# A selective scan beside two convolution stages: one projection tile a block at fixed places, and every fourth odd product on VectorE

## The chip, the cores and the metric

The kernel runs on one core of one Trainium2 chip. The metric is device time in microseconds of one launch, the median of the runs shown. A core has five engines that run side by side, each through its own queue of instructions in program order: TensorE (PE in the profile), VectorE (DVE), ScalarE (ACT), GpSimd (POOL) and SyncE (SP), whose queue issues all DMAs here. An instruction waits for semaphores that other engines' instructions raise, and whatever stands behind it in the same queue waits with it.

## The reference

Sixteen images of 64 x 64 pixels with 96 channels go through two residual layers. The first normalizes in groups, resamples by a Fourier method, applies two matrices with a quadratic between them, and resamples back. The second is a selective scan in four directions:

```python
xz = jnp.einsum('bhwc,pc->bhwp', x, in_proj_w)
xc, z = (xz[..., :d], xz[..., d:]); z = silu(z)
...
xc = silu(depthwise_conv3x3(xc) + conv_b)
xs = jnp.stack([x0, x1, x0[..., ::-1], x1[..., ::-1]], axis=1)
x_dbl = jnp.einsum('bkdl,kcd->bkcl', xs, x_proj_weight)
...
delta = jax.nn.softplus(dts + dt_bias)
def step(h, inps):
    dt, ut, bt, ct = inps
    h = jnp.exp(dt[..., None] * As) * h + (dt * ut)[..., None] * bt
    y = jnp.einsum('bkdn,bkn->bkd', h, ct)
    return h, y
```

There are 192 inner channels and 16 states a channel; the scan runs over 4096 positions. The sum of the four directions is normalized over channels, gated with z and projected back to 96 channels.

## The kernel before, in words

The work has three parts. **front** makes an image's first layer, the convolution and the silus, and leaves xs (the input of the scan) and z in HBM. **scan** is the long loop. **finish** takes the y of an image, normalizes, gates and projects it. front of image 1 runs alone, then scan over all images; front of the next image and then finish of the one before run in small steps beside the scan of an image. finish of the last image runs alone at the end.

The scan goes in 128 steps: 16 images, each with two pairs of directions (the forward pair, L807, and the backward pair, L809) and four chunks of T = 1024 positions. A step has six **blocks** (L621) of 64 channels, a block four **units** j = 0 to 3, of four states each; a unit fills 128 partitions (32 channels by four states) twice, e = 1 (odd) and e = 0 (even). So an image has 192 units and 48 blocks, and the whole 3072 units.

For a unit, `drive` (L795, GpSimd) forms b = dtu x bt over both halves; `decay` (L789, ScalarE) forms da = exp(delta x a) in PSUM, one tile for each half; `recur` (L801, VectorE) runs the scan h = da x h + b; then h is multiplied with ct, and `read_out` (L817, PE) sums over the states. The even scan writes into PSUM over da, and VectorE multiplies (L979). The odd scan has two ways. Mostly it writes into SBUF over b, and GpSimd multiplies it into a tile `odd` (L968). In some units ("odd_here", L952) it writes over da in PSUM as the even one does, and VectorE multiplies at once (L958). A credit decides: 7 are added in each unit, and at 30 a unit is taken; a unit can also be taken ahead of its turn, with 30 paid later (below). `keep` (L811) saves the last column of h for the next chunk, on VectorE for odd halves that GpSimd multiplies, on ScalarE otherwise.

Program order in a unit n: odd scan, its product or none, decay of the odd half of n + 1, slot 0, a store of y, GpSimd's odd product, drive of n + 2, even scan, read_out of n - 1, slot 1, even product, decay of the even half of n + 1, slot 2. b has four buffers, odd two, dtu two. dtu of the next block is fetched from HBM at j = 0 (L946), delta's halves at j = 1 and 2 (L948).

The **slots**, three a unit and 576 an image, hold everything else (L887). In each, `Background` (L860) compares how many steps a generator has made with its pace, and makes one if it is due: `front` and `finish` at SLICES = 499 in 576, where a step that yields HEAVY counts double, and `project` (L640) at 71 steps in 72 slots, two in a slot where a light step is late. `project` makes delta and dtu for the next step: six tiles of 128 x 512 (three channel groups v, two halves t). For each half it fetches three u, mixes them with three matmuls (pp), adds a bias (pr, L674), stores the rows of B and C, and then for each v makes a matmul s (L681), six ScalarE operations for the softplus (L689 to L696), four matmuls that add the pieces (L701), the product dtu with u on VectorE (L706), a copy of delta on ScalarE (L707), and two stores (L710, L711). pp and s share one PSUM bank.

front's convolution has 12 tiles an image. At the end of each it yields WAIT (L507); behind it stand two silus (L509, L510), with a load of their activation table in front and a load of the usual table behind (L511). Such a step is let through, a gate, at slot 2 of any unit where no store is pending; the next unit is then taken as odd_here, and for two slots `project` makes no BUSY steps.

Of the kernel before, what the change touches and what calls it, by code (L numbers as in the profile page):

```python
# [45 lines left out]
F32 = mybir.dt.float32  # L46
# [25 lines left out]
SLICES = 499  # L72
WAIT = -1
BUSY = -2
HEAVY = 2
PSLICES = 71
SHARE = 30
GAIN = 7
# [3 lines left out]
def tile_two_blocks(  # L82
# [159 lines left out]
    def front(mi):  # L242
# [227 lines left out]
        for i, n, tiles, both in ((1, 64, 4, 4), (0, 128, 8, 0)):  # L470
# [44 lines left out]
            yield HEAVY  # L515
            if i == 0:
                yield from parts(made["xs"][1], col)
            else:
                for p, t0 in halves:
                    to = made["xs"][2, 64:128, :].rearrange("c (w h) -> c w h", h=HW)  # L520
                    for w0 in range(0, HW, 16):
                        nc.sync.dma_start(
                            out=to[:, w0:w0 + 16, 8 * t0:8 * t0 + 32],
                            in_=col[p:p + n].rearrange("c (w h) -> c w h", w=HW)[:, w0:w0 + 16, :],
                        )
                        yield HEAVY

    def finish(mi):
# [16 lines left out]
        for _ in range(2):  # L545
            yield HEAVY
        tail = None
        for t in range(8):
# [7 lines left out]
            for ob, n in ((0, 128), (1, 64)):  # L556
# [26 lines left out]
                yield HEAVY  # L583
# [18 lines left out]
            yield HEAVY  # L602
# [4 lines left out]
            yield HEAVY  # L607
# [10 lines left out]
        for _ in tail:  # L618
            yield HEAVY
# [6 lines left out]
    def scan():  # L626


        with ExitStack() as es:
            pj = es.enter_context(tc.tile_pool(name="sc_pj", bufs=1))  # L630
            up_ = es.enter_context(tc.tile_pool(name="sc_u", bufs=4))
            cp = es.enter_context(tc.tile_pool(name="sc_bc", bufs=5))
# [7 lines left out]
            def project(mi, pair, lc, out, ps, half=None, own=None):  # L640

                if not out:
                    out["rows"] = dctx.tile([2, 2 * NS, T], F32, name="rows")
                    out["delta"] = [dctx.tile([128, T], F32, name=f"delta_d{v}") for v in range(3)]
                    out["dtu"] = [dctx.tile([128, T], F32, name=f"dtu_d{v}") for v in range(3)]
                    out["made"] = 0
                rows = out["rows"]  # L650
                xs_d = image[mi]["xs"]
                order = (0, 2, 1)
                halves = range(0, T, TB) if half is None else (half,)

                def make(name):
                    return own(name) if own else pj.tile([128, TB], F32, name=name)

                def fetch_u(v, t):
                    uv = own(f"u{v}") if own else up_.tile([128, TB], F32, name="u")
                    nc.sync.dma_start(out=uv, in_=xs_d[v, :, lc * T + t:lc * T + t + TB])  # L660
                    return uv

                ahead_u = [fetch_u(v, halves[0]) for v in order]
                for _ in range(4):
                    yield
                for t in halves:
                    u, ahead_u = dict(zip(order, ahead_u)), []
                    pp = ps.tile([128, TB], F32, name="pp", tag="g")
                    for v in range(3):
                        nc.tensor.matmul(pp, lhsT=xpt_s[:, pair, v, :], rhs=u[v], start=(v == 0), stop=(v == 2))  # L670
                    yield
                    yield BUSY
                    pr = make("pr")
                    nc.scalar.activation(pr, pp, AF.Identity, bias=bumps_s)  # L674


                    for i, v in enumerate(order):
                        if i == 0:
                            yield
                        s = ps.tile([128, TB], F32, name="s", tag="g")  # L680
                        nc.tensor.matmul(s, lhsT=dtw_s[:, pair, v, :], rhs=pr, start=True, stop=True)  # L681
                        if i == 0:
                            for r in range(2):
                                nc.sync.dma_start(
                                    out=rows[r, :, t:t + TB], in_=pr[64 * r:64 * r + 2 * NS, :]
                                )
                        yield BUSY
                        e, d, m, w = (make(k) for k in ("e", "d", "m", "w"))
                        nc.scalar.activation(e, s, AF.Abs)  # L689
                        nc.scalar.activation(e, e, AF.Exp, scale=-1.0)  # L690
                        yield BUSY
                        nc.scalar.activation(m, s, AF.Relu)
                        nc.scalar.activation(w, e, AF.Identity, bias=one_s)
                        yield BUSY
                        nc.scalar.activation(d, e, AF.Ln, bias=one_s)
                        nc.scalar.activation(w, w, AF.Identity, scale=-1.0, bias=one_s)  # L696
                        yield
                        s = ps.tile([128, TB], F32, name="s", tag="g")
                        yield
                        for k, of in enumerate((w, e, d, m)):  # L700
                            nc.tensor.matmul(s, lhsT=ident_s, rhs=of, start=(k == 0), stop=(k == 3))  # L701
                        for _ in range(2):
                            yield
                        yield BUSY
                        dtu, delta = make("dtu"), make("delta")
                        nc.vector.tensor_mul(dtu, s, u[v])  # L706
                        nc.scalar.copy(delta, s)  # L707
                        for _ in range(2):
                            yield
                        nc.sync.dma_start(out=out["dtu"][v][:, t:t + TB], in_=dtu)  # L710
                        nc.sync.dma_start(out=out["delta"][v][:, t:t + TB], in_=delta)  # L711
                        out["made"] += 1
                        if half is None and t + TB < T and i < 2:
                            ahead_u += [fetch_u(k, t + TB) for k in (order[:1], order[1:])[i]]
# [42 lines left out]
            far_u = b16.tile([128, 4, TB], F32, name="far_u", tag="b16")  # L757
            far_w = b18.tile([128, 6, TB], F32, name="far_w", tag="b18")
            far = {f"u{v}": far_u[:, v, :] for v in range(3)}
            far["pr"] = far_u[:, 3, :]  # L760
            far.update({k: far_w[:, i, :] for i, k in enumerate(("e", "d", "m", "w", "dtu", "delta"))})
            with tc.tile_pool(name="side_ps", bufs=4, space=PSUM) as side:
                todo = [project(*steps[0], ctxs[0], side, 0), project(*steps[0], ctxs[0], side, TB, far.get)]
                while todo:
                    todo = [g for g in todo if next(g, todo) is not todo]
                    if ctxs[0]["made"] >= 2 and not dtus:
# [93 lines left out]
            class Background:  # L860
# [11 lines left out]
                def step(self):  # L872
                    self.said = next(self.gen, 0)
                    if self.said == 0:
                        self.gen = None
                    else:
                        self.n += self.said if self.said is not None and self.said > 0 else 1
# [6 lines left out]
            ahead_gen = behind_gen = step_gen = nothing  # L884
            full, full_unit = 0, None

            def slot(position):  # L887
                nonlocal full, full_unit
                back = ahead_gen if ahead_gen.gen is not None else behind_gen
                back.at += 1  # L890
                step_gen.at += 1
                gate = back.said == WAIT and back.due() and position == 2 and storing is None
                if gate:
                    full, full_unit = 2, n + 1
                if step_gen.due() and not (full and step_gen.said == BUSY):
                    light = step_gen.said != BUSY
                    step_gen.step()

                    if light and step_gen.due() and step_gen.said != BUSY:
                        step_gen.step()  # L900
                if back.due() and (gate or back.said != WAIT):
                    back.step()
                full = max(full - 1, 0)

            last = len(units) - 1
            def next_step(st, mi):

                nonlocal step_gen
                if st < len(steps):
                    if steps[st][0] > mi:  # L910
                        ahead_gen.drain()
                    step_gen = Background(project(*steps[st], ctxs[st], gps), PSLICES, 3 * per_step)

            next_step(1, 0)
# [4 lines left out]
            storing, credit = None, 0  # L919

            for n, (st, bi, j) in enumerate(units):
# [9 lines left out]
                elif n % per_image == 2 and mi > 0:  # L931
                    behind_gen = Background(finish(mi - 1), SLICES, POS)
                if j == 0:
                    new = stp.tile([128, 2, NQ], F32, name="new", tag=f"st{bi}")
                    states[bi] = (states[bi][1] if states[bi] else None, new)

                if j == 0:
# [3 lines left out]
                    elif n + NQ <= last:  # L941
                        step_gen.drain()
                        ahead = ctxs[st + 1], 0
                        next_step(st + 2, mi)
# [6 lines left out]
                credit += GAIN  # L951
                odd_here = n == full_unit or credit >= SHARE  # L952
                if odd_here:
                    credit -= SHARE
# [158 lines left out]
```

## Time and profile before

| what | value |
|---|---|
| median of 3 runs | 20658.49 us (20655.89 to 20659.62) |
| the profiled execution | 20663.46 us |
| its span, first to last instruction | 20659.1 us |
| VectorE scans (L807, L809) | 6144 instructions, 2.28 to 2.34 us each |
| VectorE even product (L979) | 3072 x 1.223 us |
| VectorE odd product (L958) | 716 x 1.225 us |
| VectorE dtu (L706) | 765 x 0.678 us |
| ScalarE decay (L792) | 6144 x 1.116 us |
| ScalarE table loads for the silus (L509, L511) | 2 x 192, 1.283 us each |
| mean granted TensorE clock | 0.869 |

The profile comes from one execution. Its page gives, for each engine, the busy time as a share of the span; then groups of instructions by line, with the busy time, the mean of one in ns, and the idle time of the engine just before them with what ended it. Views of the trace give the waits (who waited for whom, us in total, times, longest), the instructions in order of time, and the busy time of all engines in stretches that one chooses. Two instructions of one engine can overlap by some 60 to 90 ns, so the time from start to start is a little shorter than the duration shown.

### The profile page before, as it was taken

The numbers are of one execution on the slowest core, as the hardware profiler recorded it, in microseconds if no ns is written. First come the engines' busy times: TensorE is split into PE (matmuls) and PEld (weight loads), VectorE is DVE, ScalarE is ACT, GpSimd is POOL, SyncE is SP. The second block draws the span as 40 slices with busy tenths as digits, with TensorE's granted clock in tenths as the row PEclk, the third lists the DMA queues.
The fourth block names the chain that finished last, engine by engine and source line by source line (L and its number), as shares of the span: only waits on it lengthen the run. The fifth ranks groups of instructions, "written<-read, shape, count | busy, mean of one in ns | idle before, by whom it ended". The sixth has DMA issues, their size and how long they took to land. (4 is left out here: it accounts for less than half of the span.)

```text
span 20659.1 us, 274495 instructions
## 1 busy us (share of the span) xinstructions
PE 16699.5 (81%) x98988; PEld 7144.1 (35%) x98988; DVE 19221.5 (93%) x12976; ACT 13808.3 (67%) x20655; POOL 19266.9 (93%) x5436
## 2 busy tenths in 40 slices
PE   7877888888888778888888888888888887888856
PEld 4423334233343333334333242333434333243221
DVE  0999999999999999999999999999999999999997
ACT  4766766667676776767667676676766767666653
POOL 0999999999999999999999999999999999999996
PEclk8887888988889888898888889888898888988977
DMA  2565665666666666665666666666666666666654
GB/s 82 193 210 201 202 229 202 224 205 202 229 207 226 203 218 213 207 225 199 220 216 205 225 206 221 204 209 226 205 222 205 217 212 210 223 202 220 225 191 141
DMA packets 1855472, 4277.18 MB, mean 207 GB/s; under 512 B 449438, under 2 KB 548670, under 8 KB 1852062
## 3 DMA queue, kind: packets, MB, share of 16 engines
q1 hardware_dynamic: 1854110, 4259.62, 62.4%
q8 instruction: 781, 12.80, 0.3%
q14 instruction: 581, 4.76, 0.1%
HBM read 3380.58 MB, written 878.18 MB: 206 GB/s over the span
## 5 line engine op out<-in xcount | busy, mean ns | idle before, releaser
L798 POOL TENSOR_TENSOR b<-dtu,bt 128x2048 f32<-128x2048 f32 x3072 | 13905.5, 4537 | 590.1 <-DMA dtu<-dtu_d 464.8
L792 ACT ACTIVATE da<-delta,a_s 128x1024 f32<-128x1024 f32 x6144 | 6851.8, 1116 | 2398.6 <-DVE b L979 905.6
L968 POOL TENSOR_TENSOR odd<-b,ct 128x1024 f32<-128x1024 f32 x2356 | 5569.0, 2364 | 637.5 <-DVE b L809 328.8
L979 DVE TENSOR_TENSOR b<-da,ct 128x1024 f32<-128x1024 f32 x3072 | 3757.5, 1223 | 39.2
L809 DVE TENSOR_TENSOR_SCAN da<-da,new,b 128x1024 f32<-128x1024 f32 x1408 | 3297.5, 2342 | 159.4 <-ACT da L792 133.4
L807 DVE TENSOR_TENSOR_SCAN da<-da,new,b 128x1024 f32<-128x1024 f32 x1421 | 3327.2, 2341 | 89.8 <-ACT da L792 88.1
L832 PE MATMUL y<-b,fold_s 128*32 128x256 f32 x30304 | 2589.9, 436 | 788.2 <-DVE b L979 555.5
L809 DVE TENSOR_TENSOR_SCAN b<-da,new,b 128x1024 f32<-128x1024 f32 x896 | 2098.4, 2342 | 141.5 <-POOL b L798 83.3
L807 DVE TENSOR_TENSOR_SCAN b<-da,new,b 128x1024 f32<-128x1024 f32 x883 | 2067.4, 2341 | 5.9 <-ACT da L792 5.2
L815 ACT COPY new<-da 128x1 f32<-128x1 f32 x2841 | 444.4, 156 | 2428.1 <-DVE b L979 1994.6
L491 PE MATMUL c_ps<-xgp,wtap_s 96*64 96x512 f32 (+1 forms) x4608 | 1694.5, 621 | 185.2 <-ACT row L509 179.5
L832 PE MATMUL y<-odd,fold_s 128*32 128x256 f32 x18848 | 1669.3, 429 | 153.9 <-POOL odd L968 152.3
L832 PEld LDWEIGHTS y<-b,fold_s 128*32 128x32 f32 x30304 | 723.1, 116 | 2927.0 <-issue 1246.0
L701 PE MATMUL s<-w,ident_s 128*128 128x512 f32 x1530 | 1141.5, 837 | 695.0 <-ACT w L696 618.1
L374 PE MATMUL h_ps<-xu,w1t_s 96*128 96x500 f32 x1920 | 1042.9, 643 | 215.0 <-ACT hsq L355 152.7
L681 PE MATMUL s<-pr,dtw_s 128*128 128x512 f32 x1530 | 916.9, 683 | 321.0 <-ACT delta L707 247.7
L809 DVE TENSOR_TENSOR_SCAN da<-da,b 128x1024 f32<-128x1024 f32 x486 | 1109.3, 2282 | 47.5 <-ACT da L792 44.0
L807 DVE TENSOR_TENSOR_SCAN da<-da,b 128x1024 f32<-128x1024 f32 x473 | 1079.6, 2283 | 28.1 <-ACT da L792 24.1
L386 PE MATMUL o_ps<-w2c_s,hsq 128*100 128x96 f32 x9600 | 994.3, 262 | 129.4 <-ACT hsq L355 118.9
L386 PEld LDWEIGHTS o_ps<-w2c_s,hsq 128*100 128x100 f32 x9600 | 931.9, 174 | 291.8 <-ACT hsq L355 176.5
L824 PE MATMUL y<-y,ident_s 128*128 128x512 f32 x768 | 530.8, 779 | 598.3 <-ACT yt L843 458.0
L701 PE MATMUL s<-e,ident_s 128*128 128x512 f32 x1530 | 999.8, 742 | 0.0
(145 smaller groups left out, 22946.0 us busy)
## 6 DMA issues: line engine op xcount, KB each, us to landing
dtu<-dtu_d SPq DMA_DIRECT2D x1536, 512.0 KB
delta<-delta_d SPq DMA_DIRECT2D x1536, 512.0 KB
bt<-rows SPq DMA_DIRECT2D x1024, 512.0 KB
ct<-rows SPq DMA_DIRECT2D x1024, 512.0 KB
u<-xs_d SPq DMA_DIRECT2D x893, 256.0 KB
dtu_d<-dtu SPq DMA_DIRECT2D x765, 256.0 KB
delta_d<-delta SPq DMA_DIRECT2D x765, 256.0 KB
xr<-in_x SPq DMA_DIRECT2D x768, 128.0 KB
```

The source lines that it names most:

```text
L374: nc.tensor.matmul(h_ps[j], lhsT=w1t_s[:, 128 * j:128 * (j + 1)], rhs=xu.rearrange("c p q -> c (p q)"), start=True, stop=True,)
L386: nc.tensor.matmul(o_ps[:, p, :], lhsT=hsq[j][:, UPS * p:UPS * (p + 1)], rhs=w2c_s[:, j, :], start=(j == 0), stop=(j == HB - 1),)
L491: nc.tensor.matmul(c_ps[p:p + n], lhsT=wtap_s[:, tap, 128 * i:128 * i + n], rhs=xgp[:, h0:h0 + 8, dx:dx + HW], start=(tap == 0), stop=(tap ...
L681: nc.tensor.matmul(s, lhsT=dtw_s[:, pair, v, :], rhs=pr, start=True, stop=True)
L701: nc.tensor.matmul(s, lhsT=ident_s, rhs=of, start=(k == 0), stop=(k == 3))
L792: nc.scalar.activation(da, deltas[n // NQ, e], AF.Exp, scale=a_s[:, k, g, units[n][2]:units[n][2] + 1])
L798: nc.gpsimd.tensor_mul(b, dtus[n // NQ], bt.unsqueeze(1).to_broadcast([128, 2, T]))
L807: nc.vector.tensor_tensor_scan(out, da, b, before, ALU.mult, ALU.add)
L809: nc.vector.tensor_tensor_scan(out[:, ::-1], da[:, ::-1], b[:, ::-1], before, ALU.mult, ALU.add)
L832: nc.tensor.matmul(y[32 * q:32 * q + 32, e, :], lhsT=fold_s, rhs=weighed[e][:, QT * q:QT * q + QT], start=(pair == 0 and j == 0 and e == 0 ...
L968: nc.gpsimd.tensor_mul(odds[n], h, bc[1, r, j])
L979: nc.vector.tensor_mul(bs[n][:, 0, :], h, bc[1, r, j])
```

## The change

`project` goes. Its work is cut into `task`, which makes one of the six tiles, and `mix` with `mixed` for pp and pr. Block bi < 3 makes tiles 3 to 5 of its own step, a later block tiles 0 to 2 of the next step; the order is v = 0, 2, 1 with both halves of a v in a row. The 12 slots of a block are numbered p = 0 to 11, and each piece has its fixed p: fetch of u and matmul s at 0, ScalarE at 1 to 4, the four matmuls at 6, the copy of delta at 8, dtu on VectorE at 9, the stores at 10. Blocks 2 and 3 also fetch three u at 6 for the next step's half, mix at 10, and make pr at 11. The set-up before the loop makes three tiles of step 0 instead of six.

The credit goes: odd_here is j = 3, one in each block. Its VectorE product, and the odd decay of the next unit behind it, move to behind slot 0, which holds dtu's product there. A gate opens only at slot 2 of j = 2, so that the unit behind it is an odd_here one. HEAVY goes: each step counts one. front's pace is 540 in 576; finish gets 93 steps over the positions that are left of the image when it begins, less six.

```diff
-SLICES = 499
+SLICES = 540
+FINISH = 93
...
+            prp = es.enter_context(tc.tile_pool(name="sc_pr", bufs=2))
...
-            def project(mi, pair, lc, out, ps, half=None, own=None):
...
+            tasks = [(v, t) for v in (0, 2, 1) for t in (0, TB)]
...
+            def task(st, k, ps, make):
+                v, t = tasks[k]
+                ctx, pair = ctxs[st], steps[st][1]
+                u = fetch_u(st, v, t)
+                s = ps.tile([128, TB], F32, name="s", tag="g")
+                nc.tensor.matmul(s, lhsT=dtw_s[:, pair, v, :], rhs=ctx["pr"][t], start=True, stop=True)
+                yield
+                e, d, m, w = (make(k) for k in ("e", "d", "m", "w"))
+                nc.scalar.activation(e, s, AF.Abs)
+                nc.scalar.activation(e, e, AF.Exp, scale=-1.0)
+                yield
+                nc.scalar.activation(m, s, AF.Relu)
+                nc.scalar.activation(w, e, AF.Identity, bias=one_s)
+                yield
+                nc.scalar.activation(d, e, AF.Ln, bias=one_s)
+                yield
+                nc.scalar.activation(w, w, AF.Identity, scale=-1.0, bias=one_s)
+                yield
+                yield
+                s = ps.tile([128, TB], F32, name="s", tag="g")
+                for i, of in enumerate((w, e, d, m)):
+                    nc.tensor.matmul(s, lhsT=ident_s, rhs=of, start=(i == 0), stop=(i == 3))
+                yield
+                yield
+                dtu, delta = make("dtu"), make("delta")
+                nc.scalar.copy(delta, s)
+                yield
+                nc.vector.tensor_mul(dtu, s, u)
+                yield
+                nc.sync.dma_start(out=ctx["dtu"][v][:, t:t + TB], in_=dtu)
+                nc.sync.dma_start(out=ctx["delta"][v][:, t:t + TB], in_=delta)
...
+            def block_work(st, bi, mi):
+                work = iter(())
+                if bi < 3:
+                    work = task(st, bi + 3, gps, near)
+                elif st + 1 < len(steps):
+                    work = task(st + 1, bi - 3, gps, near)
+                head = bi in (2, 3) and st + 1 < len(steps)
+                t = TB * (bi - 2)
+                for p in range(3 * NQ):
+                    next(work, None)
+                    if head and p == 6:
+                        if bi == 2:
+                            if steps[st + 1][0] > mi:
+                                ahead_gen.drain()
+                            open_step(st + 1)
+                        us = [fetch_u(st + 1, v, t) for v in range(3)]
+                    elif head and p == 10:
+                        pp = mix(st + 1, us, gps)
+                    elif head and p == 11:
+                        mixed(st + 1, t, pp)
                     yield
...
             def slot(position):
-                nonlocal full, full_unit
                 back = ahead_gen if ahead_gen.gen is not None else behind_gen
+                if back is behind_gen and back.at == 0:
+                    back.positions = 3 * (per_image - n % per_image) - 6
                 back.at += 1
-                step_gen.at += 1
-                gate = back.said == WAIT and back.due() and position == 2 and storing is None
-                if gate:
-                    full, full_unit = 2, n + 1
...
-                if back.due() and (gate or back.said != WAIT):
+                next(work, None)
+                if back.due() and (back.said != WAIT or (position == 2 and units[n][2] == NQ - 2)):
                     back.step()
...
-                    behind_gen = Background(finish(mi - 1), SLICES, POS)
+                    behind_gen = Background(finish(mi - 1), FINISH, POS)
                 if j == 0:
+                    work = block_work(st, bi, mi)
...
-                credit += GAIN
-                odd_here = n == full_unit or credit >= SHARE
-                if odd_here:
-                    credit -= SHARE
+                odd_here = j == NQ - 1
                 h = das[n, 1] if odd_here else bs[n][:, 1, :]
                 recur(n, 1, h)
                 if odd_here:
-                    nc.vector.tensor_mul(bs[n][:, 1, :], h, bc[1, r, j])
                     keep(n, 1, h, nc.scalar.copy)
-                if n < last:
+                else:
                     decay(n + 1, 1)
                 slot(0)
+                if odd_here:
+                    nc.vector.tensor_mul(bs[n][:, 1, :], h, bc[1, r, j])
+                    if n < last:
+                        decay(n + 1, 1)
```

## The prediction

> **What bounds the kernel now.** I read the page's busy table first, then the groups, then the waits of VectorE and GpSimd, and last stretches of one image.
>
> ```profile
> PE 16699.5 (81%) x98988; PEld 7144.1 (35%) x98988; DVE 19221.5 (93%) x12976; ACT 13808.3 (67%) x20655; POOL 19266.9 (93%) x5436
> L798 POOL TENSOR_TENSOR b<-dtu,bt 128x2048 f32<-128x2048 f32 x3072 | 13905.5, 4537 | 590.1 <-DMA dtu<-dtu_d 464.8 <-PE y L832 94.8 <-DMA bt<-rows 26.9
> L968 POOL TENSOR_TENSOR odd<-b,ct 128x1024 f32<-128x1024 f32 x2356 | 5569.0, 2364 | 637.5 <-DVE b L809 328.8 <-PE y L832 85.9 <-issue 80.2
> ```
>
> VectorE and GpSimd are both 93% busy, and neither starts before the set-up is over: the first scan starts at 492.65 us, the last ends at 20494.8, and finish of the last image takes the 164 us behind it. In the 20002 us between, VectorE is idle for some 810 us and GpSimd for some 760. Two engines are nearly full and feed each other, so I count what each must do per block of four units, from starts in the timeline:
>
> ```profile
> 8005.44 2.34 DVE L809 TENSOR_TENSOR_SCAN b<-da,new,b 128x1024 f32<-128x1024 f32 x1
> 8007.69 2.33 DVE L809 TENSOR_TENSOR_SCAN da<-da,new,b 128x1024 f32<-128x1024 f32 x1
> 8010.06 1.23 DVE L979 TENSOR_TENSOR b<-da,ct 128x1024 f32<-128x1024 f32 x1
> 8011.20 2.29 DVE L807 TENSOR_TENSOR_SCAN da<-da,b 128x1024 f32<-128x1024 f32 x1
> ...
> 8005.50 4.54 POOL L798 TENSOR_TENSOR b<-dtu,bt 128x2048 f32<-128x2048 f32 x1
> 8009.99 2.38 POOL L968 TENSOR_TENSOR odd<-b,ct 128x1024 f32<-128x1024 f32 x1
> 8012.30 9.02 POOL L798 TENSOR_TENSOR b<-dtu,bt 128x2048 f32<-128x2048 f32 x2
> ```
>
> From start to start: scan 2.25, scan whose result the next instruction reads 2.37, multiply 1.14, drive 4.49, GpSimd's odd product 2.31. Now one image (number 6 of 16), in blocks 0 to 26 (front's main part), 27 to 35 (its convolution) and 36 to 47 (finish); the fourth row is the last image, which has no front beside it:
>
> ```profile
> core 0: us, PE busy (x) PEld busy (x) DVE busy (x) ACT busy (x) POOL busy (x), PEclk, DMA share, GB/s
> 6759.80:7441.50 681.70, 538.76 (x3990) 269.82 (x3992) 665.78 (x448) 489.72 (x777) 675.54 (x192) 0.85 0.61 204
> 7441.50:7688.40 246.90, 206.12 (x974) 75.79 (x970) 226.53 (x155) 182.07 (x250) 218.66 (x61) 0.91 0.64 209
> 7688.40:8011.20 322.80, 283.87 (x1224) 93.13 (x1224) 307.45 (x210) 189.31 (x265) 308.63 (x89) 0.93 0.72 235
> 19287.00:20494.80 1207.80, 761.57 (x3904) 252.45 (x3904) 1191.88 (x797) 672.93 (x950) 1196.45 (x339) 0.76 0.56 191
> ```
>
> GpSimd lacks 6 us in the first stretch, 28 in the second, 14 in the third, 11 in the image without front: the convolution is where the time goes. Its gates put two odd products on VectorE in one block and none in a later one, and the table loads behind them make VectorE wait for decays. The waits:
>
> ```profile
> DVE dtu L706 <- PE s L701: 342.6, 128, 156.7
> DVE da L809 <- ACT da L792: 177.3, 150, 7.7
> DVE b L809 <- POOL b L798: 85.1, 125, 1.1
> ACT delta L707 <- DVE dtu L706: 480.1, 227, 6.2
> ```
>
> 157 of the first 343 us are one wait in the set-up. ScalarE is held too: its copy of delta stands behind VectorE's product on the same PSUM tile.
>
> **The odd products.** 716 are on VectorE now (7 of 30, and those that gates force); then it is one in each block, 768. GpSimd loses 52 x 2.31 = 120 us. VectorE gains 52 x 1.14 = 59 us, and loses 39 of the 1767 copies of L815 (0.13 each, 5 us). A block then costs GpSimd 4 x 4.49 + 3 x 2.31 = 24.9 us, an image 48 x 24.9 = 1195. VectorE: three units of 2.25 + 2.37 + 1.14 = 5.76, and the fourth 2.25 + 0.60 (product, from start to start) + 1.14 + 2.37 + 1.14 = 7.50: 24.8. So outside finish GpSimd is the bound by a hair. Can they run in step? Behind the end of a block's first odd scan GpSimd needs 6.8 us for each of three units against VectorE's 5.76, so it falls back by 3.1 us and wins it back in the fourth. A drive has to end before the odd scan two units later starts; the tightest place, the fourth unit, leaves 1.4 us. A spacing of five leaves 0.3, which is why the dealing of now pays small waits on both sides. The fixed four absorbs jitter of a microsecond.
>
> **The product behind the odd scan.** dtu now stands three positions behind its matmuls and one behind the copy of delta, so the waits L706 <- PE (186 us outside the set-up) and L707 <- DVE (480 us of ScalarE) should go. It also fills the space between scan and dependent multiply. [...] In the fourth unit the next odd decay now waits for slot 0 and the multiply. Behind it on ScalarE stand slot 1's pieces, keep and the even decay. It has 2.37 + 1.14 us until the next odd scan and needs 1.12: hidden. Without that cover it would cost its 1.12 in 768 units, 860 us.
>
> **Steps at fixed places.** Six tiles a step as before, the same ScalarE and PE instructions; at most 1.3 us of ScalarE in a position (Abs and Exp 0.58 + 0.63; Relu and Identity 0.58 + 0.71). Between the odd decay and the even one there is room for some 2.4 us and 0.9 of slack. The SP queue: the stores of a tile at place 10, the fetch of u at place 0, the mixes' three u at place 6 (four places, some 9 us, before PE reads them). In three of six blocks the tile just stored is fetched by the very next SP work, dtu for the block after. Before its first drive there are 20.6 us. At the start of the scan, in a quiet queue, the store left at 456.55 and the drive began at 465.85: 9.3 us. In a busy one, from the semaphore updates, a pair of fetches lands in 7.1 us (98th percentile 15), a store in 2.1 (7): hidden except beside s<-s_d, some 4% of the time. Below nothing isn't possible here; above, one miss of 5 us an image. I take 1. The set-up makes three tiles, not six; a pair takes 16.6 us there (452.45, 468.87, 485.63), so the scan starts at 476.
>
> **The gates.** Front's 359 steps at 540 per 576 positions reach the first wait at about position 296, and then a gate opens once in 12 positions, always with the fourth unit next. Table loads, silus and the second load (1.28 + 0.69 + 0.59 + 1.28 = 3.8 us) start about 2 us behind the third unit's last multiply and end at 5.9; the next odd decay isn't wanted before 11, the even one before 9.9. So the table loads' share of VectorE's waits for decays (157 of 370 us, by what ScalarE did before each) goes. What is late next is PE. After a gate front takes five steps in five positions. By starts in the trace a convolution step takes 1.87 us, a read-out 2.1, the matmul of s 1.1. From the silu's end at 4.05: four steps, two read-outs, one s end at 16.8, and the drive that needs the buffer wants it at 17.9. With the mix (3.2 us, in blocks 2 and 3, some 4 of 12 gates) it is 2.1 late; at a clock 15% lower 0.8 and 4.5. I take 0.4 for eight gates and 3 for four: 15 us an image, against 27 now. The nearest row for both ends: none late (0), all at the low clock (24). [...] The rows show 0.85 to 0.93 granted; at half the chain ends at 29.6, 11.7 late. I take the rows.
>
> **Finish** has 90 steps. Front ends near position 446, so they get some 123 positions, 0.73 a position (now 0.62, heavier steps counted double). Its 24 products of 0.6 us are VectorE's: 14 us in which it, not GpSimd, is the bound. I take 13, between 11 (slack absorbs some) and 18 (with ycol's loads in a row holding up other fetches once, as now).
>
> **Sum** of an image: 1195 + 3 (front's main part, 6 now) + 15 + 13 = 1226, against 1252 for images 2 to 15. 14 x 1226 = 17164; the first, without finish, 1221 (1256); the last 1201 (1208); 476 before, 164 after: 20226, 433 less than the span of 20659.1. The profiled execution took 20663.5, 5 more than the median of 20658.5, so I forecast 20225.
>
> **Rivals.** First, PE keeps up and only the ties remain: 1195 + 0 + 3 + 12 = 1210, 20000 us. For it: the last image, 5 us over its count. Against: PE 83% busy in the convolution. Second, the waits move: convolution and finish cost what they cost now (27 and 15), front 5: 1242, 20450. For it: VectorE and GpSimd tie, and each late read-out also holds ScalarE's Abs and so the even decay. Third, on the other side: PE's bursts run at the lower clock and GpSimd stops for buffers behind every gate, 15 x 12 = 180 of them. Without the gates' price the sum is 20016; from 3.8 us a gate the change is slower. At 5 us: 20916. A third of the bursts at half clock would do it. Against: now the same waits (L798 and L968 <- PE y) are 181 us in all. That the change doesn't do what it says: gates that never open would leave front to be drained at once; the count of positions excludes it.
>
> **Numbers.** Forecast 0.57 (own range 20080 to 20400), first rival 0.12, second 0.13, third 0.14, no change 0.04. Some 0.2% is what a measurement tells from no change. So faster 0.82, same 0.04, slower 0.14. The range 19990 to 20600 leaves out the third rival and no change.
>
> **What would show it.** 768 odd products on VectorE and 2304 on GpSimd; no waits of dtu's product on PE; decays' waits at gates near zero; images of about 1226 us and a last one near 1201; GpSimd idle mostly for PE's y behind gates. Odd scans that wait for drives in every block, or GpSimd waits for y over 500 us, would make it wrong.

## The result, and the profile after

| kernel | median, us | ratio to before, 95% interval |
|---|---|---|
| before | 20657.19 | |
| changed | 21295.54 (21270.29 to 21311.97) | 1.0308 (1.029 to 1.0326) |

The change makes the kernel slower by 3.1%. Forecast were 20225, range 19990 to 20600, with 0.14 for slower. The median of before is here over four executions, the three shown above and one more; each experiment's ratio is to executions of the kernel before that were made beside it (medians 20654 to 20661). The line numbers of the changed kernel differ: the odd product on VectorE is L964, keep L838, the decay L815, dtu's product L699, the copy of delta L697, GpSimd's odd product L972.

First the busy table and two groups of the page of the changed kernel; the groups' last part is the idle time of the engine just before them and what ended it.

```profile
span 21310.2 us, 275957 instructions
...
PE 16984.3 (80%) x98988; PEld 7259.9 (34%) x98988; DVE 19225.2 (90%) x12989; ACT 13817.4 (65%) x20694; POOL 19149.8 (90%) x5384
...
L972 POOL TENSOR_TENSOR odd<-b,ct 128x1024 f32<-128x1024 f32 x2304 | 5437.2, 2360 | 1488.4 <-DVE b L832 579.2
...
L964 DVE TENSOR_TENSOR b<-da,ct 128x1024 f32<-128x1024 f32 x768 | 934.4, 1217 | 746.0 <-ACT new L838 745.6
```

The work is as forecast: 768 odd products on VectorE, 2304 on GpSimd, GpSimd busy 117 us less. VectorE's instructions take 48 us more in sum, but they overlap more, so that its busy time rises by only 4. What grew is idle time: between first and last scan VectorE now idles 1469 us where it was 809. The last group says where; in the kernel before it had 49 us of idle time:

```profile
L958 DVE TENSOR_TENSOR b<-da,ct 128x1024 f32<-128x1024 f32 x716 | 877.0, 1225 | 49.0 <-DVE da L809 0.9
```

The waits of VectorE in the changed kernel (us in total, times, longest):

```profile
DVE b L964 <- ACT new L838: 745.6, 255, 5.5
DVE dtu L699 <- ACT delta L697: 557.6, 189, 159.9
...
DVE sq L602 <- PE o_ps L597: 87.5, 68, 2.9
...
DVE da L830 <- ACT da L815: 78.3, 111, 1.5
...
DVE b L830 <- ACT da L815: 37.9, 35, 6.0
DVE da L832 <- ACT da L815: 15.3, 30, 1.0
...
DVE b L832 <- ACT da L815: 3.2, 9, 0.4
```

The waits for decays did fall, from 371 us to 135. Two new ones are larger: the odd product waits for ScalarE's copy of a single column, and dtu's product for ScalarE's copy of delta (557.6, of which 160 are one wait in the set-up). One gate shows how. VectorE and then ScalarE in order of time, in the convolution beside the first image's scan; an engine's idle time stands in brackets:

```profile
1296.86 2.35 DVE L832 TENSOR_TENSOR_SCAN da<-da,new,b 128x1024 f32<-128x1024 f32 x1
1299.12 0.67 DVE L699 TENSOR_TENSOR dtu<-s,u 128x512 f32<-128x512 f32 x1
1302.79 1.22 DVE L964 TENSOR_TENSOR b<-da,ct 128x1024 f32<-128x1024 f32 x1 [3.00 <-ACT new L838]
...
1298.23 0.58 ACT L697 COPY delta<-s 128x512 f32<-128x512 f32 x1
1298.82 1.28 ACT L505 ACT_TABLE_LOAD   x1
1300.12 0.69 ACT L505 ACTIVATE row<-c_ps,convb_s 128x512 f32<-128x512 f32 x1
1300.70 0.59 ACT L506 ACTIVATE z<-z_ps 128x512 f32<-128x512 f32 x1
1301.31 1.28 ACT L507 ACT_TABLE_LOAD   x1
1302.60 0.16 ACT L838 COPY new<-da 128x1 f32<-128x1 f32 x1
```

The scan is done at 1299.2, dtu's product at 1299.8, and then VectorE stands still for 3.00 us. Its product reads da in PSUM; so does keep's copy, and keep comes first in the program. The two are put in order by a wait, although both only read. The copy takes 0.16 us, but it stands in ScalarE's queue behind 3.8 us of silus and table loads. In the kernel before the product came first, and it was the copy on ScalarE that waited, 424 us in all, on an engine that was busy for only 67% of the span:

```profile
ACT new L815 <- DVE b L958: 424.0, 294, 3.4
```

### The profile page after: what moved, and what is told of

Read it like the earlier page. It is cut to its first block, busy times and chain, and to the rows that moved or that the text cites. A ratio compares the mean times of both kernels' runs of the same rounds, so it can differ in the third digit from the quotient of the medians.

```text
span 21310.2 us, 275957 instructions
## 1 busy us (share of the span) xinstructions
PE 16984.3 (80%) x98988; PEld 7259.9 (34%) x98988; DVE 19225.2 (90%) x12989; ACT 13817.4 (65%) x20694; POOL 19149.8 (90%) x5384
## 3 DMA queue, kind: packets, MB, share of 16 engines
q1 hardware_dynamic: 1964702, 4461.00, 62.4%
## 5 line engine op out<-in xcount | busy, mean ns | idle before, releaser
L815 ACT ACTIVATE da<-delta,a_s 128x1024 f32<-128x1024 f32 x6144 | 6861.5, 1117 | 2900.1 <-DVE b L983 929.9
L972 POOL TENSOR_TENSOR odd<-b,ct 128x1024 f32<-128x1024 f32 x2304 | 5437.2, 2360 | 1488.4 <-DVE b L832 579.2
L983 DVE TENSOR_TENSOR b<-da,ct 128x1024 f32<-128x1024 f32 x3072 | 3760.0, 1224 | 41.9
L855 PE MATMUL y<-b,fold_s 128*32 128x256 f32 x30720 | 2683.0, 445 | 1245.2 <-DVE b L983 643.7
L830 DVE TENSOR_TENSOR_SCAN da<-da,new,b 128x1024 f32<-128x1024 f32 x1440 | 3369.9, 2340 | 38.5 <-ACT da L815 37.7
L832 DVE TENSOR_TENSOR_SCAN da<-da,new,b 128x1024 f32<-128x1024 f32 x1440 | 3368.7, 2339 | 3.9 <-ACT da L815 3.9
L487 PE MATMUL c_ps<-xgp,wtap_s 96*64 96x512 f32 (+1 forms) x4608 | 1944.2, 693 | 684.1 <-ACT row L505 678.3
L838 ACT COPY new<-da 128x1 f32<-128x1 f32 x2880 | 453.8, 158 | 2568.3 <-DVE b L983 2492.2
L830 DVE TENSOR_TENSOR_SCAN b<-da,new,b 128x1024 f32<-128x1024 f32 x864 | 2022.8, 2341 | 20.5 <-ACT da L815 20.5
L832 DVE TENSOR_TENSOR_SCAN b<-da,new,b 128x1024 f32<-128x1024 f32 x864 | 2021.9, 2340 | 3.2 <-ACT da L815 3.2
L964 DVE TENSOR_TENSOR b<-da,ct 128x1024 f32<-128x1024 f32 x768 | 934.4, 1217 | 746.0 <-ACT new L838 745.6
L487 PEld LDWEIGHTS c_ps<-xgp,wtap_s 96*64 96x64 f32 (+1 forms) x4608 | 631.2, 185 | 1696.5 <-issue 920.5
L382 PE MATMUL o_ps<-w2c_s,hsq 128*100 128x96 f32 x9600 | 1053.7, 270 | 133.3 <-ACT hsq L351 132.6
L382 PEld LDWEIGHTS o_ps<-w2c_s,hsq 128*100 128x100 f32 x9600 | 987.1, 182 | 357.9 <-ACT hsq L351 178.1
L832 DVE TENSOR_TENSOR_SCAN da<-da,b 128x1024 f32<-128x1024 f32 x480 | 1094.2, 2280 | 11.4 <-ACT da L815 11.4
```

The lines of the kernel that those rows point to most:

```text
L382: nc.tensor.matmul(o_ps[:, p, :], lhsT=hsq[j][:, UPS * p:UPS * (p + 1)], rhs=w2c_s[:, j, :], start=(j == 0), stop=(j == HB - 1),)
L487: nc.tensor.matmul(c_ps[p:p + n], lhsT=wtap_s[:, tap, 128 * i:128 * i + n], rhs=xgp[:, h0:h0 + 8, dx:dx + HW], start=(tap == 0), stop=(tap ...
L815: nc.scalar.activation(da, deltas[n // NQ, e], AF.Exp, scale=a_s[:, k, g, units[n][2]:units[n][2] + 1])
L830: nc.vector.tensor_tensor_scan(out, da, b, before, ALU.mult, ALU.add)
L832: nc.vector.tensor_tensor_scan(out[:, ::-1], da[:, ::-1], b[:, ::-1], before, ALU.mult, ALU.add)
L855: nc.tensor.matmul(y[32 * q:32 * q + 32, e, :], lhsT=fold_s, rhs=weighed[e][:, QT * q:QT * q + QT], start=(pair == 0 and j == 0 and e == 0 ...
```

## The experiments

Two theories to begin with. **Theory 1**: the change turned round the order of two engines that read one PSUM tile, in two places (keep and odd product; delta and dtu), and so moved waits from ScalarE, which has time, to VectorE, which has none. **Theory 2**: the fixed gates and the denser pace make PE and ScalarE late in any order, and the order only decides where the wait shows.

**keep behind the product.** In the changed kernel:

```diff
                 if odd_here:
-                    keep(n, 1, h, nc.scalar.copy)
-                else:
+                if not odd_here:
                     decay(n + 1, 1)
                 slot(0)
                 if odd_here:
                     nc.vector.tensor_mul(bs[n][:, 1, :], h, bc[1, r, j])
+                    keep(n, 1, h, nc.scalar.copy)
```

> The changed kernel with one edit: in the fourth unit keep (ScalarE's copy of the last column of da) stands behind VectorE's odd product instead of in front of it. Theory 1, the order of two readers of one PSUM tile: the product no longer waits for the copy, so its 746 us of waits fall below 50, and the time falls by 550 to 750, to some 20550 to 20750. Theory 2, gates and front's denser pace make PE and ScalarE late whatever the order, and the wait is only where it shows: the wait comes back at decays or at GpSimd's waits for y, and the time stays above 21100.

Measured: 20966.39, ratio 1.015 (1.0134 to 1.0165). 329 us come back, less than theory 1 said, and the time is below theory 2's bound. The product's wait is gone from the list of VectorE's waits, whose head is now

```profile
DVE dtu L699 <- ACT delta L697: 635.7, 205, 160.1
DVE xgp L457 <- PE e_ps L445: 256.3, 1, 256.3
DVE da L832 <- ACT da L815: 221.2, 111, 3.0
...
DVE b L832 <- ACT da L815: 67.6, 40, 2.2
```

The other pair's wait grew by 78 us, and the backward scans' waits for decays from 18 to 289 us (the two lines of L832 together): ScalarE's lateness, no longer met at L964, is met in part at the next place. So neither forecast came out whole: a part of the wait came back at the decays, as theory 2 has it.

**dtu in front of delta.** In the changed kernel:

```diff
-                nc.scalar.copy(delta, s)
                 yield
                 nc.vector.tensor_mul(dtu, s, u)
+                nc.scalar.copy(delta, s)
                 yield
```

> The changed kernel with one edit: the copy of delta on ScalarE stands behind dtu's product on VectorE (both read the same s in PSUM), as before the change. Theory 1: the 390 us that dtu's product waits for the copy inside the scan go, ScalarE waits instead, and the time falls by 250 to 400, to some 20900 to 21050. Theory 2: no change over 100 us.

Measured: 21162.99, ratio 1.0251 (1.0234 to 1.0268), 133 us less: more than theory 2 allows, less than theory 1 hoped. dtu's wait for ScalarE is gone (390 of its 398 us inside the scan stood behind a decay, by what ScalarE did just before the copy), but L964 waits 879 us where it waited 746:

```profile
DVE b L964 <- ACT new L838: 879.0, 359, 6.2
```

**Both.**

> The changed kernel with both edits. Theory 1: VectorE's waits for ScalarE's copies go, and what the forecast counted remains: 20200 to 20450, faster than the kernel before. Theory 2: above 20900.

Measured: 20644.74, ratio 0.9996 (0.9988 to 1.0005). The two edits together give back 651 us, more than the 329 and 133 they give alone: with one pair mended, the other pair's wait grew (by 78 us and by 133). Between first and last scan VectorE idles 812 us, as in the kernel before (809). So the two orders make all of the loss against the kernel before, for the fixed gates and the denser pace are still there. But the forecast of 20225 isn't reached (theory 1 said 20200 to 20450): 420 us are left. What VectorE waits for now (its list of waits, parts of it):

```profile
DVE dtu L698 <- PE s L693: 254.6, 110, 159.8
...
DVE da L832 <- ACT da L815: 183.6, 113, 3.0
DVE da L830 <- ACT da L815: 138.7, 196, 1.5
...
DVE sq L602 <- PE o_ps L597: 100.5, 64, 2.9
```

Decays again (463 us in four lines; 135 in the changed kernel, where VectorE had already waited elsewhere), and two products for PE: dtu's, 95 us of it inside the scan, and one in finish.

**The opposite edit in the kernel before**: keep in front of the odd product, nothing else.

```diff
                 if odd_here:
+                    keep(n, 1, h, nc.scalar.copy)
                     nc.vector.tensor_mul(bs[n][:, 1, :], h, bc[1, r, j])
-                    keep(n, 1, h, nc.scalar.copy)
```

> The kernel before with the opposite edit: keep stands in front of the odd product on VectorE (L958), nothing else. Theory 1: each of the 716 products waits for ScalarE, at least 0.3 us for the copy itself (215 us) and some 2 us behind each of 180 gates' table loads (360 us): 21100 to 21350, slower than before. Theory 2: within 100 us of before.

Measured: 21207.44, ratio 1.0266 (1.0251 to 1.0282): two lines of program order cost 553 us, without fixed places, new gates or denser pace. With this and the version before it theory 2 falls as the cause of the loss. The head of VectorE's waits of this kernel:

```profile
DVE b L959 <- ACT new L815: 893.5, 536, 6.6
DVE dtu L706 <- PE s L701: 279.3, 82, 157.7
```

By what ScalarE did just before the copy, 639 of the 894 us stand behind the silus' table loads.

**The copy on VectorE, at the same place.** The changed kernel with `nc.vector.tensor_copy` for `nc.scalar.copy` in keep of the fourth unit.

> The changed kernel with one edit: in the fourth unit keep stays in front of the odd product, but VectorE makes the copy. Theory 1, order of readers on two engines: the place is the same, but there is no other engine's queue in front of it, so the product's waits for a copy go as in e1_keep_after (20966); 576 copies more on VectorE at some 0.15 us cost at most 85 us, so 20900 to 21050. If it is the place of the copy and not the engine's queue, the waits stay and the time is above 21250.

Measured: 20970.17, ratio 1.0153 (1.0136 to 1.017), the same as with keep behind the product. No wait of L964 is left in VectorE's list, whose head is

```profile
DVE dtu L699 <- ACT delta L697: 549.3, 202, 159.4
```

So it is not the place of the copy but the other engine's queue in front of it.

**What is left above the forecast.** From the starts of the scans, mean of images 2 to 15, in us for stretches of blocks (front's main part, its convolution in the changed kernels, finish), the first image, which has no finish beside it, and the last (to the end of its last scan), which has no front:

| kernel | 0-23 | 24-36 | 37-47 | first image | last image |
|---|---|---|---|---|---|
| before | 608.9 | 352.4 | 291.5 | 1255.8 | 1207.9 |
| changed | 636.5 | 361.5 | 301.9 | 1271.2 | 1198.8 |
| both orders turned | 615.6 | 337.1 | 302.6 | 1229.7 | 1197.9 |
| forecast (blocks of 24.9, and 3, 15 and 13 on top) | 601 | 339 | 287 | 1221 | 1201 |

The convolution is what the forecast has; front's main part and finish are not. Two theories: a place (one of the slots) too close behind another (**theory 3**), or the density of the background steps (**theory 4**).

**Abs one place later** (and the four matmuls with it, at 7), on the kernel with both orders turned:

```diff
                 nc.tensor.matmul(s, lhsT=dtw_s[:, pair, v, :], rhs=ctx["pr"][t], start=True, stop=True)
                 yield
+                yield
...
                     nc.tensor.matmul(s, lhsT=ident_s, rhs=of, start=(i == 0), stop=(i == 3))
                 yield
-                yield
```

> The changed kernel with both orders turned round (as e3_both_after), and Abs, Exp and what follows one place later (2 to 5), the four matmuls at 7. What is left above the forecast in e3_both_after is 410 us. Theory 3, a fixed place too close behind another: Abs stands one place behind its matmul, a late PE holds it, and the even decay behind it makes VectorE wait (150 us in 75 waits behind Abs and Exp); with a place between, 100 to 170 us go, to 20470 to 20550. Theory 4, density: the same steps of front and finish are packed closer (540 and 93 in the rest, against 499 with heavy steps double); then nothing over 50 us.

Measured: 21388.51, ratio 1.0355 (1.034 to 1.037), 744 us slower than without, against what both theories said. VectorE's first wait tells why:

```profile
DVE dtu L698 <- PE s L694: 1168.5, 411, 158.7
```

With two places between the four matmuls and dtu's product PE is late in 410 tiles of 767; with three it was in 109 (95 us). I had counted what the added place gives at Abs, not what it takes at the product. The waits for decays do fall, from 463 to 287 us, but they fell in the changed kernel too, where VectorE already waited elsewhere. A version with the place in front of Abs and three behind the matmuls was not run, so theory 3 stays open at Abs.

**A free place in finish**, where the heavy mark was:

```diff
-FINISH = 93
+FINISH = 101
...
                 nc.tensor.matmul(o_ps, lhsT=ow_s[0:n, i, :], rhs=yz[i], start=(i == 0), stop=(i == 1))
             yield
+            yield
             e_ps = bank([C, TB], "oe_ps")
```

> As e3_both_after, with an empty step in finish between o_ps and the product that reads it (where the heavy mark was), 101 steps for 93. Theory 3: the product's waits (139 us) fall below 60, the time by 50 to 90. Theory 4: finish is denser still, its blocks get longer, and the time stays or rises by up to 50.

Measured: 20519.54, ratio 0.9934 (0.9918 to 0.9951), faster than before. Blocks 37 to 47 take 294.3 us instead of 302.6; the product's wait for o_ps falls from 100.5 to 22.9 us:

```profile
DVE sq L603 <- PE o_ps L597: 22.9, 8, 2.9
```

The sign and the wait are theory 3's, and theory 4's is ruled out: the removed mark had been a place of waiting. The gain of 125 us is more than the 50 to 90 that theory 3 said; what the rest comes from was not taken apart.

**Both gaps.**

> As e3_both_after with both gaps. Theory 3: the two gains add, 20400 to 20480, below the kernel before by about 1%. Theory 4: above 20580.

Measured: 21248.56, ratio 1.0287 (1.0272 to 1.0303). Against theory 3, the two gains do not add; theory 4's bound holds, but not for its reason. The free place in finish gives 140 us here too, and the loss at dtu's product (1082 us of waits for PE, 160 of them in the set-up) stands beside it.

**front at 499 in 576.**

> As e3_both_after with front at 499 in 576. The first image, which has no finish, is read alone: 1229.7 us in e3_both_after, of which its first 24 blocks take some 24 us more than 24 x 24.8. Theory 4: these 24 blocks lose at least 8 us of that. Theory 3: less than 4. The whole run gets slower in both, 20750 to 21100, since finish is left about as many places as it has steps.

Measured (one execution, so without an interval): 20810.36. The first image takes 1219.1 us, its first 24 blocks 610.1 instead of 620.0, the mean over the later images 607.2 instead of 615.6, as theory 4 said (at least 8). Finish, with some 87 places for its 90 steps, takes 325.5 instead of 302.6.

**Room for finish.** Two stores of col to a step behind the fourth gate save one gate's round, 12 places; and then front runs at three paces.

```diff
-                        yield
+                        if w0 % 32:
+                            yield
```

> As e6_finish_gap, and the eight stores of col behind the fourth gate go two to a step, so that the next tile of the convolution reaches the next gate and not the one behind it: front ends 12 places earlier, and finish has 135 places for its 98 steps where it had 123. Theory 4, density: blocks of finish get some 4 us an image shorter, 20440 to 20480. If not density but single steps of finish set its price, no change over 25 us.

> As e9_merged_stores with front at 564 in 576, so that the first gate is a block earlier (place 284) and finish has 147 places. Theory 4: front's main part gets some 3 us an image longer, finish some 3 us shorter: within 40 us of e9_merged_stores. If single steps set the price, both stay.

> As e9_merged_stores with front at 520 in 576 (first gate at place 308, finish has 123 places, as in e6_finish_gap). Theory 4: front's main part 4 to 6 us an image shorter than in e6_finish_gap, finish as there: within 60 us of e9_merged_stores.

| front in 576 | places for finish | 0-23 | 37-47 | median, us | ratio |
|---|---|---|---|---|---|
| 564 | 147 | 625.9 | 288.1 | 20674.27 | 1.0007 (0.9997 to 1.0016) |
| 540 | 135 | 615.8 | 292.1 | 20482.82 | 0.9914 (0.9899 to 0.9929) |
| 520 | 123 | 611.2 | 293.7 | 20460.34 | 0.9902 (0.9887 to 0.9917) |

The directions are theory 4's throughout, the sizes only in part. The merged stores gave 37 us, 2 an image in finish where theory 4 said 4. At 520 it came out as said. At 564 the time is 191 us above the version at 540, where at most 40 were said: front's main part loses 10 us an image, not 3, and blocks 24 to 36 (where finish already begins) 6 (342.1 for 336.4).

The first 24 blocks do not hold the same work at every pace, since a slower front makes fewer steps in them. The first gate falls in block 26, 25, 24 and 23 (counted from 0) at 499, 520, 540 and 564, and ahead of that block front makes about 270 steps in each. These stretches take 10, 13, 18 and 28 us an image more than 24.9 a block, so the same steps did cost more where they stood closer. The clock granted to TensorE in them (0.82, 0.84, 0.83, 0.83) does not go with it. Whether it is density as such or single steps that meet bad places isn't shown: which step meets which place changes with the pace, and that was not taken apart further. The version at 520 is the fastest seen, 1% under the kernel before: both orders turned, the free place, the merged stores.

## Why the prediction was wrong, point by point

- **The work of a block** (24.8 us on VectorE, 24.9 on GpSimd, in step at a spacing of four): right. The last image, without front, takes 1198.8 us from its first scan to the last scan's end, in the stretch of the trace of the changed kernel:

```profile
core 0: us, PE busy (x) PEld busy (x) DVE busy (x) ACT busy (x) POOL busy (x), PEclk, DMA share, GB/s
...
19945.60:21144.40 1198.80, 783.69 (x3940) 261.41 (x3940) 1193.02 (x801) 688.63 (x980) 1188.22 (x335) 0.78 0.60 205
```

  1201 was forecast, and 1207.9 was the kernel before's. VectorE's waits for drives, 123 us before, are 5. One reading was off: between first and last scan of the kernel before GpSimd idles 741 us; the 760 count from its first drive.
- **"The product behind the odd scan": the step that failed**, twice, and it makes 651 of the 1071 us between the forecast and the measured time. It said that the waits of dtu's product would go, since it stands one place behind the copy of delta; and of the fourth unit it named only the decay as held. keep, moved in front of the product, was counted nowhere. The prediction had shown the line ACT delta L707 <- DVE dtu L706, 480 us, and had even said that both read one PSUM tile. What the line means it did not draw: the two readers of the tile are kept in the order of the program (ScalarE waited 480 us in 227 times), and the second waits for all that stands in the first one's queue (3.00 us at the gate above). The trace of before had the other pair too, in ScalarE's 424 us of waits for L958. Moving delta and keep in front turned both waits round. dtu's product, which was to wait no more, got 398 us for ScalarE in place of its 186 for PE; and half of those for PE were only hidden behind them, since with the orders turned 95 us of them show. That there is such an order between two reads is what L964's wait shows (745.6 us in 255 times); what it is for isn't shown, and no run here tried it without.
- **The dependent product.** With the orders turned the odd product starts 0.59 us behind dtu's product, as counted (0.60), and the 48 us of idle time behind the scan are gone. The count of VectorE's block takes 2.25 us from a scan's start to an independent successor's and 2.37 to a dependent one's, and the trace of the changed kernel has them again (medians of 2.26 and 2.37): an independent successor starts before the scan's own 2.28 to 2.34 us are over.
- **"Steps at fixed places"**: the set-up ends as forecast (first scan at 476.8, forecast 476), and the stores just ahead of their fetches held up no drive. The forecast overlooked that u is now fetched once for the mix and once more for the tile: 1664 loads for 893, 201 MB more in all; the queue's share stays at 62.4%, and no wait of VectorE or GpSimd for u shows.
- **"The gates"**: silus and tables end when forecast. In the changed kernel no wait for a decay stands behind them (157 us before); keep is what they hold, 582 of the 746 us by what ScalarE did just before it. With the orders turned 58 us of decay waits come back there, some 4 an image, where the forecast had none. The 15 us an image fit in sum with the orders turned (337.1 against 13 x 24.9 = 323.7), but that they are PE's lateness, as the forecast has it, isn't shown.
- **Finish and front's main part** were mis-sized: 13 and 3 us an image forecast, 29 and 18 with the orders turned (302.6 less 11 x 24.9; 615.6 less 24 x 24.9). These 31 us over 14 images are some 430, about the 420 us that stay above the forecast. The forecast took the heavier marks for mere counting; taking one of them away cost finish 8 us an image, and front's steps cost 8 more at 540 than at 499.
- **The rivals.** The slower one had the right direction for another reason: it had PE's bursts at a low clock. The clock granted does fall to 0.50 for some microseconds (7498 to 7506 us in the kernel before), but its mean in the convolution of image 6 fell only from 0.91 to 0.87, and GpSimd's waits for PE's y are 67 us in all (181 before), so it was not that. A rival "ScalarE's queue is put in front of VectorE" was missing.

## What to carry to other kernels

Where two engines read one PSUM tile and a trace shows one of them waiting for the other, as it did here in both pairs (480 and 424 us in the kernel before), count them as dependent, and let the engine that is full read first: here the second reader inherited all that stood in the first one's queue, 3.8 us of silus and table loads in front of a copy of 0.16. Before moving an instruction of an idle engine forward, ask who waits for it. And when one of two such waits is mended, expect less until the other is too: 329 and 133 us alone were 651 together.

## What the runs showed of the hardware that was not expected

In this kernel one place more or less between matmuls and their reader decides: with two places of some 2.1 us (24.9 us over 12) VectorE waited 1010 us for PE inside the scan, with three 95, for the same work of PE. And the price of background work rose with its pace beside two nearly full engines: the same 270 or so steps of front cost 10, 13, 18 and 28 us an image above the scan's own 24.9 a block at 499, 520, 540 and 564 steps in 576 places (at 499 in one execution).
